# One token tile's query product ahead of the first scores, three tiles' in one row behind them

## The chip, the core and the metric

The kernel runs on one core of one Trainium2 chip. The metric is the device time of one execution in microseconds; the lower the better. Before the change it was 635.88 us, the median of three runs (635.7 to 636.29).

A core has a matrix engine (PE in the profile, with its weight loads shown apart as PEld), a vector engine (DVE), a scalar engine (ACT), a general engine (POOL) and an engine that only issues transfers (SP). Each takes its own instructions in the order in which the program gives them and waits on semaphores for the others.

## What is computed

Eight sequences of 64 tokens, 512 wide, go through three residual blocks: a cross attention against eight contexts of 1601 rows, a linear-attention block with its MLP, and a mixture of eight experts. The change lies in the first block:

```
p       = layernorm(x)                      # 8*64 tokens x 512
trans_q = ctx @ W.T + b                     # never formed: folded into the query
scores  = p @ trans_q.T                     # = (p @ W) @ ctx.T + p @ b
att     = softmax(scores) @ ctx
x       = x + relu(att @ W.T + b)
...                                         # linear attention, MLP, experts
```

The kernel forms `p @ W` once (the query product, `pw_t`) and multiplies it with the context's rows; `p @ b` is one number for each token (`pb`) and comes in as the bias of the copy that takes the scores out of the accumulator banks. All of it is float32.

## The kernel before

**Tiles.** The 512 tokens are four tiles of 128 (two sequences each), numbered t = 0 to 3. The inner dimension 512 is four pieces of 128. The contexts' rows are taken as scores in four groups g of 401 or 398 keys, and as values in three groups of 512 rows and a tail.

**Order.** The order on PE, DVE, ACT, POOL and SP is the order of the program text: it is scheduled by hand, nothing is reordered. Dependences are kept by regions of a tile: a reader of token tile 0 of a buffer does not wait for a later write of tile 1.

**Loads.** x comes in two halves of two tiles, on SP's and on ACT's queue (`xs`, line 101). Then SP loads W (`w_sb`, line 113) and after it everything else in one list (`stream`, `issue_to`): the keys of tile 0, group by group (`ctxT`, two loads of 0.8 MB each, one for each sequence), the bias b after the first group, then keys and rows (`ctx`, two loads of 1 MB) in the order of their use. Context loads go into a ring of 12 buffers (`RING`), and SP issues one when the buffer's former content has been used. Loads also share eight completion semaphores in turn, so that each waits for the landing of the one eight places ahead.

**Start of the work.** Twelve idle matmuls on `ident` (line 224) come first on PE. For each pair of tiles, `statistics` (DVE, then a square root on ACT) and `normalize` (DVE) write `pn`, which is the buffer `xin`; `turn_p` transposes a tile on PE and ACT copies it to `p_t`, which is the buffer `h_t`. W is transposed into four banks (line 405), copied by DVE to `w_t` (line 411); `w_t` is first used at line 547. `pw_half` makes the query product of two tiles for one piece `hc`, 256 columns a matmul, copied by ACT. The first half of the query product lies ahead of the first scores, the second half among the four score groups of tile 0:

```python
    for g in range(4):
        key_group(0, g)
        pw_half(1, g)
```

`key_group(t, g)` (line 441) is the scores of one tile against one group, with ACT's copy under the bias `pb[:, t]`; after g = 3, `softmax` follows. `pb` is computed on DVE after the W copies (line 421). From there `turn_scores` (line 474), `weigh` (line 502, scores times rows), `attended` (line 544) and the later tiles' `key_group`s alternate on PE, with the next block's `values` (line 575) among them.

PSUM is held as two sets of four banks, `mm_bank` and `acc_bank`, given out in turn.

Of the kernel before, what the change touches and what calls it, by code (L numbers as in the profile page):

```python
# [20 lines left out]
P = 128  # L21
B, S, D = 8, 64, 512
LK = 1601
NT = B * S // P
KC = D // P
# [23 lines left out]
def perceiver_kernel(  # L49
# [22 lines left out]
    nc = tc.nc  # L72
# [11 lines left out]
    def mm_bank(name):  # L84
        return ps.tile([P, 512], F32, tag="mm", name=name)

    def acc_bank(name):
        return ps.tile([P, 512], F32, tag="acc", name=name)
# [8 lines left out]


    xs = resid.tile([P, NT, D], F32, name="xs")
    for t, queue in ((0, nc.sync), (2, nc.scalar)):  # L100
        queue.dma_start(xs[:, t : t + 2, :], x[:, t : t + 2, :])
    moe = ctx.enter_context(tc.tile_pool(name="moe", bufs=1))
    mid = ctx.enter_context(ExitStack())
    xinp = mid.enter_context(tc.tile_pool(name="xinp", bufs=1))
# [6 lines left out]
    xa2 = xas.enter_context(tc.tile_pool(name="xa2", bufs=2))  # L111
    w_sb = xa.tile([P, KC, D], F32, tag="w", name="w_sb")
    nc.sync.dma_start(w_sb, xw)
    w_t = xa.tile([P, KC, D], F32, name="w_t")
    xb_bc = const.tile([P, D], F32, name="xb_bc")


    half = H * DH // 2
# [99 lines left out]

    ident = const.tile([P, P], F32, name="ident")
# [133 lines left out]
    def statistics(src, name):  # L353
        st = small.tile([P, 6], F32, tag="st", name=f"st_{name}")
        nc.vector.bn_stats(st, src)
        mv = small.tile([P, 2], F32, tag="mv1", name=f"mv_{name}")
        nc.vector.bn_aggr(mv, st)
        std = small.tile([P, 1], F32, tag="std1", name=f"std_{name}")
        nc.scalar.activation(std, mv[:, 1:2], AF.Sqrt, bias=eps)
        return mv, std  # L360

    def normalize(dst, src, mv, std, name):

        rstd = small.tile([P, 1], F32, tag="rstd1", name=f"rstd_{name}")
        nc.vector.reciprocal(rstd, std)
        nc.vector.tensor_scalar(dst, src, mv[:, 0:1], rstd, ALU.subtract, ALU.mult)


    pn, p_t = xin, h_t
    def turn_p(t):  # L370
        bank = mm_bank(f"tr_p_{t}")
        for c in range(KC):
            nc.tensor.transpose(bank[:, c * P : (c + 1) * P], pn[:, t, c * P : (c + 1) * P], ident)
        nc.scalar.copy(p_t[:, :, t * P : (t + 1) * P], bank.rearrange("p (c q) -> p c q", c=KC))


    pw_t = xa.tile([P, KC, B * S], F32, name="pw_t")

    def pw_half(half, hc):
        cols = slice(half * 2 * P, (half + 1) * 2 * P)  # L380
        bank = mm_bank(f"pw_{half}_{hc}")
        for oc in range(KC):
            nc.tensor.matmul(
                bank[:, : 2 * P],
                w_sb[:, oc, hc * P : (hc + 1) * P],
                p_t[:, oc, cols],
                start=(oc == 0),
                stop=(oc == KC - 1),
            )
        nc.scalar.copy(pw_t[:, hc, cols], bank[:, : 2 * P])  # L390

    issue_to(len(order))

    for t in range(0, NT, 2):
        of = [statistics(xs[:, t + h, :], f"p_{t + h}") for h in range(2)]
        for h in range(2):
            normalize(pn[:, t + h, :], xs[:, t + h, :], *of[h], f"p_{t + h}")
        if t == 0:
            turn_p(0)
            turn_p(1)  # L400

            w_banks = [acc_bank(f"w_t_{hc}") for hc in range(KC)]
            for hc in range(KC):
                for oc in range(KC):
                    nc.tensor.transpose(
                        w_banks[hc][:, oc * P : (oc + 1) * P], w_sb[:, oc, hc * P : (hc + 1) * P], ident
                    )
    pw_half(0, 0)
    pw_half(0, 1)
    for hc in range(KC):  # L410
        nc.vector.tensor_copy(w_t[:, hc, :], w_banks[hc])
    turn_p(2)
    turn_p(3)
    pw_half(0, 2)
    pw_half(0, 3)

    nc.vector.stream_shuffle(xb_bc, xb_in, [0] * 32)
    pb = xa.tile([P, NT], F32, name="pb")
# [22 lines left out]
    def key_group(t, g):  # L441

        if t >= NT:
            return
        if g == 0:
            all_scores[t] = xa2.tile([P, LK], F32, tag="scores", name=f"scores_{t}")
        width = WIDTHS[g]
        sc = acc_bank(f"sc_{t}_{g}")
        keys = [need("ctxT", t, g, h) for h in range(2)]
        for c in range(KC):  # L450
            for h in range(2):
                nc.tensor.matmul(  # L452
                    sc[h * S : (h + 1) * S, :width],
                    pw_t[:, c, (2 * t + h) * S : (2 * t + h + 1) * S],
                    keys[h][:, c, :],
                    start=(c == 0),
                    stop=(c == KC - 1),
                )
        done(*[("ctxT", t, g, h) for h in range(2)])
        nc.scalar.activation(  # L460
            all_scores[t][:, g * SW : g * SW + width], sc[:, :width], AF.Identity, bias=pb[:, t : t + 1]
        )
        if g == 3:
            softmax(t)

    def softmax(t):
        scores = all_scores[t]
        negmax = small.tile([P, 1], F32, tag="negmax", name=f"negmax_{t}")
        nc.vector.tensor_reduce(negmax, scores, AX.X, ALU.max, negate=True)
        rowsum = small.tile([P, 1], F32, tag="rowsum", name=f"rowsum_{t}")  # L470
        nc.scalar.activation(scores, scores, AF.Exp, bias=negmax, accum_out=rowsum)
        all_rinv[t] = rowsum
# [129 lines left out]
            ALU.add,  # L602
        )

    for g in range(4):
        key_group(0, g)
        pw_half(1, g)
    for g in range(2):
        key_group(1, g)
    for t in range(NT):  # L610
# [43 lines left out]
    if True:  # L654
# [178 lines left out]
        of = join(0), join(1)  # L833
# [3 lines left out]
        of = join(2)  # L837
# [7 lines left out]
        of = join(3)  # L845
# [228 lines left out]
    t = NT - 1  # L1074
# [51 lines left out]
    bank = acc_bank("counts")  # L1126
# [632 lines left out]
```

## Time and profile before

| what | value |
|---|---|
| median of three runs | 635.88 us |
| the profiled execution | 636.05 us |
| its span, first to last instruction | 634.3 us |
| PE busy | 617.5 us, 97% |
| DVE, ACT, POOL busy | 29%, 19%, 10% |
| first instruction of real work on PE (`turn_p(0)`) | 8.42 us |
| first scores on PE | 20.66 us |
| start of `turn_scores(0)` on PE | 45.29 us |
| bytes moved | 131.74 MB, mean 208 GB/s over the span |

The profile gives times from the span's start. A float32 matmul shows as two records, a transpose as one. The profile models the end of a matmul, so the pace is read from start to start. PEclk is the clock that the matrix engine was granted, as a share of full speed.

### The profile page before, as it was taken

The page shows a single profiled execution, that of the slowest core. Times are in us where ns is not written, and L with a number is a line of the kernel's source. Part 1 is how long each engine was busy: PE and PEld are TensorE (multiplying, and loading weights), DVE is VectorE, ACT ScalarE, POOL GpSimd, SP SyncE. Part 2 cuts the span into 40 slices and gives each one's busy share as a digit, 9 for nine tenths or more (in the row PEclk, how much of TensorE's full clock was granted, in tenths as well). Part 3 has the DMA queues.
Part 4 walks back from the last instruction along what each step waited for, and adds up shares of the span by engine and source line. Part 5 has one row for each costly group of instructions (what it writes and reads, how often), then busy time and mean ns, then how long its engine had stood idle before and what let it go on. Part 6 is the DMA issues. An engine that isn't in the chain of part 4 may idle for free. (4 is left out here: it accounts for less than half of the span.)

```text
span 634.3 us, 8728 instructions
## 1 busy us (share of the span) xinstructions
PE 617.5 (97%) x3572; PEld 352.2 (56%) x3572; DVE 182.8 (29%) x433; ACT 120.0 (19%) x225; POOL 64.1 (10%) x87
## 2 busy tenths in 40 slices
PE   7999999999999999999999999999999999999994
PEld 7653434343444444455444447966783667775793
DVE  5111322333326888670000026501311101011100
ACT  2241332320132122031111111301101101111110
POOL 4000000000000000050000002241210121301100
PEclk8999999999999999999999999999999999999998
DMA  8999999999421203030312121426890477784711
GB/s 352 409 422 425 423 422 423 425 428 421 199 67 57 77 2 134 0 132 1 122 35 109 67 100 67 168 79 240 300 367 3 165 295 272 298 327 143 296 19 17
DMA packets 23617, 131.74 MB, mean 208 GB/s; under 512 B 4068, under 2 KB 4068, under 8 KB 12168
## 3 DMA queue, kind: packets, MB, share of 16 engines
q1 hardware_dynamic: 19064, 121.80, 48.5%
q0 software_dynamic: 3248, 7.58, 4.8%
q10 hardware_dynamic: 1248, 1.59, 0.8%
q8 instruction: 38, 0.62, 0.4%
q14 instruction: 19, 0.16, 0.1%
HBM read 126.05 MB, written 4.91 MB: 206 GB/s over the span
## 5 line engine op out<-in xcount | busy, mean ns | idle before, releaser
L1261 PEld LDWEIGHTS up<-xgT,e_up 128*128 128x128 f32 x896 | 100.7, 192 | 4.5 <-ACT y_sb L1239 2.5
L1261 PE MATMUL up<-xgT,e_up 128*128 128x128 f32 x896 | 101.6, 275 | 1.0 <-PEq L1589 0.6
L1227 DVE TENSOR_TENSOR mid<-up,act 128x256 f32<-128x256 f32 x38 | 16.1, 425 | 149.2 <-ACT act L1225 149.2
L1275 PE MATMUL y<-e_wo,mid 128*128 128x512 f32 (+1 forms) x144 | 58.8, 547 | 0.0
L858 PE MATMUL hid<-v_sb,w 128*128 128x512 f32 (+2 forms) x144 | 56.6, 545 | 0.0
L879 PE MATMUL mlp<-w,hid_sb 128*128 128x512 f32 x112 | 51.0, 597 | 0.0
L452 PE MATMUL sc<-ctxT,pw_t 128*64 128x401 f32 (+1 forms) x256 | 46.1, 503 | 0.0
L513 PE MATMUL av<-ctx,eT 128*64 128x512 f32 x192 | 43.5, 597 | 0.0
L858 PEld LDWEIGHTS hid<-v_sb,w 128*128 128x128 f32 x144 | 26.2, 190 | 29.1 <-issue 27.3
L1225 ACT ACTIVATE act<-up 128x256 f32<-128x256 f32 x38 | 14.6, 384 | 120.5 <-PE up L1261 96.7
L1275 PEld LDWEIGHTS y<-e_wo,mid 128*128 128x128 f32 x144 | 25.7, 190 | 20.5 <-issue 17.8
L1240 POOL DMA_INDIRECT out_dram<-y_sb,dst_late x12 | 18.3, 1528 | 166.8 <-ACT y_sb L1239 96.8
L879 PEld LDWEIGHTS mlp<-w,hid_sb 128*128 128x128 f32 x112 | 20.7, 190 | 23.5 <-issue 23.4
L873 POOL TENSOR_TENSOR xin<-xin,b_bc 128x512 f32<-128x512 f32 x4 | 5.1, 1268 | 268.4 <-DVE rstd_h L815 265.0
L452 PEld LDWEIGHTS sc<-ctxT,pw_t 128*64 128x64 f32 x256 | 17.5, 136 | 26.0 <-issue 25.8
L666 PE MATMUL wk<-h_t,wk 128*128 128x512 f32 x64 | 29.5, 604 | 0.0
L666 PE MATMUL wq<-h_t,wq 128*128 128x512 f32 x64 | 29.4, 602 | 0.0
L583 PE MATMUL v<-wv,h_t 128*128 128x512 f32 x64 | 29.2, 599 | 0.0
L777 PE MATMUL wo<-wo,a_t 128*128 128x512 f32 x64 | 28.9, 599 | 0.0
L927 DVE TENSOR_TENSOR xs<-mlp,xs 128x512 f32<-128x512 f32 x3 | 2.1, 691 | 86.5 <-PE mlp L879 86.5
L751 DVE RECIPROCAL rden<-rden 128x512 f32<-128x512 f32 x8 | 26.8, 3353 | 0.3
L513 PEld LDWEIGHTS av<-ctx,eT 128*64 128x64 f32 x192 | 13.0, 136 | 24.2 <-issue 23.9
(263 smaller groups left out, 627.8 us busy)
## 6 DMA issues: line engine op xcount, KB each, us to landing
e_up<-in_L_ffn_up_dram SPq DMA_DIRECT2D x32, 1024.0 KB, 5.3
ctx<-in_ctx_dram SPq DMA_DIRECT2D x24, 1024.0 KB, 17.3
ctxT<-in_ctx_T_dram SPq DMA_DIRECT2D x24, 802.0 KB, 13.3
e_wo<-in_L_ffn_wo_dram SPq DMA_DIRECT2D x16, 1024.0 KB, 10.3
w<-in_L_attn_w_dram SPq DMA_DIRECT2D x8, 1024.0 KB, 6.9
ctxT<-in_ctx_T_dram SPq DMA_DIRECT2D x8, 796.0 KB, 16.2
wv<-in_L_attn_wv_dram SPq DMA_DIRECT2D x2, 1024.0 KB
wq<-in_L_attn_wq_dram SPq DMA_DIRECT2D x2, 1024.0 KB, 17.8
```

The costliest lines, as they stand in the source:

```text
L452: nc.tensor.matmul(sc[h * S : (h + 1) * S, :width], pw_t[:, c, (2 * t + h) * S : (2 * t + h + 1) * S], keys[h][:, c, :], start=(c == 0), s ...
L513: nc.tensor.matmul(av[h * S : (h + 1) * S, :], e_t[:, 4 * g + j, h * S : (h + 1) * S], rows[h][:, j, :], start=(g == 0 and j == 0), stop=F ...
L583: nc.tensor.matmul(bank, h_t[:, c, t * P : (t + 1) * P], wv_n[:, c, :], start=(c == 0), stop=(c == KC - 1))
L666: nc.tensor.matmul(bank, w[:, c, (j % 4) * P : (j % 4 + 1) * P], h_t[:, c, :], start=(c == 0), stop=(c == KC - 1),)
L751: nc.vector.reciprocal(rden, rden)
L777: nc.tensor.matmul(wo_banks[t], a_t[:, j, t * P : (t + 1) * P], wo_r[j // 4][:, j % 4, :], start=(j == 0), stop=(j == nj - 1),)
L858: nc.tensor.matmul(hid_banks[f][:, tokens], w[:, c, (f % 4) * P : (f % 4 + 1) * P], h2_t[:, c, tokens], start=(c == 0), stop=(c == KC - 1),)
L879: nc.tensor.matmul(acc[t], hid[:, t * P : (t + 1) * P], need("w2", f // 4)[:, f % 4, :], start=(f == 0), stop=(f == FF // P - 1),)
L1227: nc.vector.tensor_tensor(hid, bank[:, FQ:], act, ALU.mult)
L1240: nc.gpsimd.indirect_dma_start(out=out, out_offset=bass.IndirectOffsetOnAxis(ap=dst[:n, :], axis=0), in_=y_sb[:n, :], in_offset=None, boun ...
L1261: nc.tensor.matmul(bank[:, m * P : (m + 1) * P], up_of[q][:, c, m * P : (m + 1) * P], xg_t[c], start=(c == 0), stop=(c == KC - 1),)
L1275: nc.tensor.matmul(bank[:, :width], h_t[:, j * P : (j + 1) * P], w[:, 2 * (q % 2) + j, n * width : (n + 1) * width], start=(q + j == 0), s ...
```

## The change

- x is loaded in two other parts: token tile 0 alone, ahead of W, and tiles 1 to 3 in one load behind W. Both are on SP's queue; ACT issues none.
- Statistics and normalisation go tile by tile, each with its own trip to ACT, in place of two tiles side by side.
- After tile 0 is normalised, only `turn_p(0)`, the query product of tile 0 (`query(hc, 0, 1)`, 128 columns a matmul) and half of W's transposes (`turn_w(0)`, `turn_w(1)`, copied by ACT) lie ahead of the first scores.
- `key_group(0, 0)` comes next, then `turn_p` of tiles 1 to 3, then `key_group(0, 1)`, then the query product of tiles 1 to 3 in one row (`query(hc, 1, 3)`, 384 columns a matmul), then the other half of W's transposes (copied by DVE), then groups 2 and 3 of tile 0.

```diff
-    for t, queue in ((0, nc.sync), (2, nc.scalar)):
-        queue.dma_start(xs[:, t : t + 2, :], x[:, t : t + 2, :])
+    nc.sync.dma_start(xs[:, :1, :], x[:, :1, :])
...
     nc.sync.dma_start(w_sb, xw)
+    nc.sync.dma_start(xs[:, 1:, :], x[:, 1:, :])
...
-    def pw_half(half, hc):
...
+    def query(hc, first, n):
+        cols = slice(first * P, (first + n) * P)
+        bank = mm_bank(f"pw_{first}_{hc}")
         for oc in range(KC):
             nc.tensor.matmul(
-                bank[:, : 2 * P],
+                bank[:, : n * P],
                 w_sb[:, oc, hc * P : (hc + 1) * P],
                 p_t[:, oc, cols],
...
+        nc.scalar.copy(pw_t[:, hc, cols], bank[:, : n * P])
+
+    def turn_w(hc, copy):
+        bank = acc_bank(f"w_t_{hc}")
+        for oc in range(KC):
+            nc.tensor.transpose(bank[:, oc * P : (oc + 1) * P], w_sb[:, oc, hc * P : (hc + 1) * P], ident)
+        copy(w_t[:, hc, :], bank)
...
-    for t in range(0, NT, 2):
-        of = [statistics(xs[:, t + h, :], f"p_{t + h}") for h in range(2)]
-        for h in range(2):
-            normalize(pn[:, t + h, :], xs[:, t + h, :], *of[h], f"p_{t + h}")
+    for t in range(NT):
+        normalize(pn[:, t, :], xs[:, t, :], *statistics(xs[:, t, :], f"p_{t}"), f"p_{t}")
         if t == 0:
             turn_p(0)
-            turn_p(1)
-
-            w_banks = [acc_bank(f"w_t_{hc}") for hc in range(KC)]
             for hc in range(KC):
-                for oc in range(KC):
-                    nc.tensor.transpose(
-                        w_banks[hc][:, oc * P : (oc + 1) * P], w_sb[:, oc, hc * P : (hc + 1) * P], ident
-                    )
-    pw_half(0, 0)
-    pw_half(0, 1)
-    for hc in range(KC):
-        nc.vector.tensor_copy(w_t[:, hc, :], w_banks[hc])
-    turn_p(2)
-    turn_p(3)
-    pw_half(0, 2)
-    pw_half(0, 3)
+                query(hc, 0, 1)
+            for hc in range(2):
+                turn_w(hc, nc.scalar.copy)
...
-    for g in range(4):
+    key_group(0, 0)
+    for t in range(1, NT):
+        turn_p(t)
+    key_group(0, 1)
+    for hc in range(KC):
+        query(hc, 1, NT - 1)
+    for hc in range(2, KC):
+        turn_w(hc, nc.vector.tensor_copy)
+    for g in range(2, 4):
         key_group(0, g)
-        pw_half(1, g)
```

More of the change, by code (lines that the diff above doesn't have):

```diff
@@ L377, in perceiver_kernel @@
     pw_t = xa.tile([P, KC, B * S], F32, name="pw_t")
-    def pw_half(half, hc):
-        cols = slice(half * 2 * P, (half + 1) * 2 * P)
-        bank = mm_bank(f"pw_{half}_{hc}")
+    def query(hc, first, n):
+        cols = slice(first * P, (first + n) * P)
+        bank = mm_bank(f"pw_{first}_{hc}")
         for oc in range(KC):
             nc.tensor.matmul(
-                bank[:, : 2 * P],
+                bank[:, : n * P],
                 w_sb[:, oc, hc * P : (hc + 1) * P],
@@ L389, in pw_half @@
             )
-        nc.scalar.copy(pw_t[:, hc, cols], bank[:, : 2 * P])
+        nc.scalar.copy(pw_t[:, hc, cols], bank[:, : n * P])
[4 more added lines that the diff above has]
+        copy(w_t[:, hc, :], bank)
     issue_to(len(order))
-    for t in range(0, NT, 2):
-        of = [statistics(xs[:, t + h, :], f"p_{t + h}") for h in range(2)]
-        for h in range(2):
-            normalize(pn[:, t + h, :], xs[:, t + h, :], *of[h], f"p_{t + h}")
+    for t in range(NT):
+        normalize(pn[:, t, :], xs[:, t, :], *statistics(xs[:, t, :], f"p_{t}"), f"p_{t}")
         if t == 0:
             turn_p(0)
-            turn_p(1)
-            w_banks = [acc_bank(f"w_t_{hc}") for hc in range(KC)]
             for hc in range(KC):
-                for oc in range(KC):
-                    nc.tensor.transpose(
-                        w_banks[hc][:, oc * P : (oc + 1) * P], w_sb[:, oc, hc * P : (hc + 1) * P], ident
-                    )
-    pw_half(0, 0)
-    pw_half(0, 1)
-    for hc in range(KC):
-        nc.vector.tensor_copy(w_t[:, hc, :], w_banks[hc])
-    turn_p(2)
-    turn_p(3)
-    pw_half(0, 2)
-    pw_half(0, 3)
+                query(hc, 0, 1)
+            for hc in range(2):
+                turn_w(hc, nc.scalar.copy)
     nc.vector.stream_shuffle(xb_bc, xb_in, [0] * 32)
```

## The prediction, made before the changed kernel ran

> **What bounds the kernel now.** I read the page first, then PE's timeline up to the first softmax, the early stretches in windows, and last the transfers of the scores' stage.
>
> ```profile
> span 634.3 us, 8728 instructions
> PE 617.5 (97%) x3572; PEld 352.2 (56%) x3572; DVE 182.8 (29%) x433; ACT 120.0 (19%) x225; POOL 64.1 (10%) x87
> ...
> DMA  8999999999421203030312121426890477784711
> ```
>
> PE is the bound nearly everywhere, so what PE saves early arrives at the end, unless something else ends last in between. The DMA row names the candidate: the transfers are full for ten slices, to about 165 us. PE's timeline:
>
> ```profile
> 1.45 4.78 PE L224 MATMUL idle<-ident 128*128 128x128 f32 x24 [1.45 <-POOL ident masks.py:199]
> 8.42 1.77 PE L373 MATMUL tr_p<-ident,xin 128*128 128x128 f32 x8 [2.20 <-DVE xin L366]
> 9.98 2.97 PE L405 MATMUL w_t<-ident,w_sb 128*128 128x128 f32 x16
> 12.78 3.62 PE L383 MATMUL pw<-h_t,w_sb 128*128 128x256 f32 x16
> 16.24 1.04 PE L373 MATMUL tr_p<-ident,xin 128*128 128x128 f32 x8
> 17.11 3.62 PE L383 MATMUL pw<-h_t,w_sb 128*128 128x256 f32 x16
> 20.66 2.92 PE L452 MATMUL sc<-ctxT,pw_t 128*64 128x401 f32 x16
> 23.51 1.99 PE L383 MATMUL pw<-h_t,w_sb 128*128 128x256 f32 x8
> ...
> 39.74 5.62 PE L452 MATMUL sc<-ctxT,pw_t 128*64 128x401 f32 x32
> 45.29 1.53 PE L485 MATMUL et<-ident,scores 128*128 128x128 f32 x12
> ...
> 85.69 2.85 PE L452 MATMUL sc<-ctxT,pw_t 128*64 128x398 f32 x16
> ```
>
> PE waits once, 2.2 us for tile 0's normalised rows, and is dense from 8.42 us. Columns of the windows: busy us and records of PE, PEld, DVE, ACT, POOL, then granted clock, DMA share, GB/s.
>
> ```profile
> 5.31:8.72 3.41, 1.21 (x11) 1.02 (x11) 2.55 (x8) 0.59 (x2) 2.41 (x13) 1.00 1.02 427
> 8.72:12.13 3.41, 3.41 (x19) 3.23 (x18) 2.86 (x9) 1.55 (x4) 0.00 (x0) 0.50 1.02 424
> 623.12:626.53 3.41, 2.36 (x11) 1.73 (x10) 0.48 (x1) 0.47 (x1) 0.00 (x0) 1.00 0.00 0
> 626.53:629.94 3.41, 0.00 (x0) 0.00 (x0) 0.00 (x0) 0.00 (x0) 1.55 (x1) 1.00 0.34 27
> ```
>
> The stretch behind the wait runs at half clock: 3.41 us that do 1.7 us of work. The last two rows are the counterexample: a stretch with 2.36 us busy did not lower the next.
>
> The transfers, in SP's timeline and in its waits from 82 to 85 us:
>
> ```profile
> 64.32 2.81 SPq L201 DMA_DIRECT2D ctxT<-in_ctx_T_dram  x2
> ...
> 84.34 0.33 SPq L201 DMA_DIRECT2D ctx<-in_ctx_dram  x1
> ```
>
> ```profile
> SPq L201 <- DMA ctxT<-in_ctx_T_dram: 3.0, 2, 1.5
> ```
>
> The keys of group (2, 3) are the two issues from 64.32 us. SP's issue at 84.34 waited for the landing of the second, so that came at 84.3. PE uses it at 85.69. Followed over every key and row load up to 165 us in this way, this is the least slack: 1.4 us.
>
> **The change, step by step.** All durations are of this execution; I follow it to the start of `turn_scores(0)`, 45.29 before.
>
> *Tile 0's load.* A lone 1 MB load on an idle SP queue (`e_up`, issued at 241.7) lands after 4.8 us. Tile 0 has 0.79 MB less, 1.85 us at 424 GB/s: 2.95 us, so about 3.8. [...] The upper bound is the old landing, 6.0. I take 3.8, the nearest row. DVE and ACT then need, by the first tile's rows without the second tile between, 0.73 (statistics), 0.21, 0.32 (root on ACT), 0.17, 0.61 (normalise, handoff): 2.04, so 5.9. The idle matmuls end at 6.1, so PE starts there in both cases: 2.3 us earlier than 8.42.
>
> *The first row.* Four transposes at 0.11 (eight took 16.24 to 17.11), ACT's copy 0.59 and the handoffs: `query` starts at 7.5, PE idle 0.9. W lands before that: it landed at 8.5 and has 0.79 MB less ahead, 6.6. 32 records of 128 columns at 0.11 (the 128 records of L1261 from 604.04 take 14.53): 3.6, to 11.1. Eight transposes of W, 0.9: 12.0. The first keys have the same bytes ahead as before and land at 12.4 (SP's issue at 12.46 waited for them): scores from 12.45, 2.85 a group (20.66 to 23.51), to 15.3. PE idle 0.4.
>
> *Tiles 1 to 3.* On ACT the root of tile 1 now lies behind the four query copies and two W copies: it starts at 12.7. Tile 1 is normalised at 13.8, and each next tile takes a whole trip, 0.69 + 0.22 + 0.33 + 0.66 = 1.9: 15.7 and 17.6. On PE, `turn_p(3)` waits for that, 1.4 us idle. Group (0, 1) follows, 18.15 to 21.0. DVE's shuffle (0.76) and first bias column (0.70) end at 19.1; ACT's first score copy waits for it, and behind it in ACT's order stand the three `p_t` copies (0.48 apart): 21.2. So the row starts at 21.3, 0.3 idle.
>
> *The row and the rest.* 32 records of 384 columns: the pace is 0.216 at 256 columns and 0.429 at 512, so 0.322, 10.3 us, to 31.6. W's other transposes 0.9, then four groups as before (two took 39.74 to 45.29 with the switch, two more 5.4): `turn_scores(0)` at 43.5. **Gain on PE: 1.8 us.** As an account: start 2.3, half clock gone 1.7, fewer switches between 64 and 128 columns 0.7 (0.34 a pair, from the 4.78 us period less 2.70 and 1.73), query product 13.9 against 13.8, new idle time 3.0: 1.6, which agrees to 0.2.
>
> *Costed at nothing.* SP's extra x issue (0.44) moves the key issues, covered by a queue in which the first key load waits 8.6 us; uncovered it costs 0.44. ACT's x issue goes, in its idle start. W's late halves are first used at 70 us. `softmax(0)` has lost the query product behind group (0, 3): its exponential ends at 42.4, 1.1 us ahead of need, and beyond that it costs one for one.
>
> *A rule against the row.* "TensorE: Matmul & The Clock Gate" (HAM oscillation) warns of idle gaps over about 3.4 us. By that neither the old gap of 2.2 us nor the new one of 1.4 lowers the clock, the half-clock stretch has another cause and may stay: the gain would be 0.1. In the row a gap of 2.2 is followed by 0.50. I go by the row: it goes with the gap.
>
> *What is late next.* PE would reach group (2, 3) at 83.9, but its keys land at 84.3 whatever PE does: the stream before it has the same bytes and starts as early. With a handoff of 0.06 and a first record 0.06 longer PE keeps 1.3 us, 1.4 if SP's first packet is slightly ahead of ACT's old one. I take 1.4. The later slacks (2.1 us and more) then hold, and PE carries it to the end.
>
> The profiled execution was 636.05 us, its span 634.3 and 1.75 around it, 0.17 above the median: 634.65 against it, **634.5 against the median**.
>
> **Rivals.**
>
> 1. *The stream does not bind.* The new start lets it run 0.4 us ahead. Then the whole 1.8 us stays: 634.1. Against it: DMA share 1.01 to 1.03 from 5 us on leaves nothing to catch up.
> 2. *The clock falls in the new wait.* The 1.4 us for tile 3 in one stretch leave about 2.1 us busy, between 1.21 (fell) and 2.36 (did not). It costs 1.7 us: 635.8, no change.
> 3. *Slower: the normalisation chain starves PE.* Tiles 1 to 3 make three trips DVE, ACT, DVE one after the other, behind ACT's copies. The price is the lateness of tile 3 one for one, and from about 0.7 us of it the stretch falls under 1.5 us busy and half clock adds 1.7. It decides at 1.4 us, 0.47 a trip: 1.8 - 1.4 - 1.7 = -1.3, so 637.2, and at 2.4 us 638.2. For it: handoffs are priced at 0.03 to 0.05 us each, with no room. Against it: DVE and ACT have nothing else to do there.
>
> **How the numbers follow.** The likeliest case (0.60) is a gain of 0.9 to 2.0 us, 633.9 to 635.0. What a measurement tells from no change is 0.2%, 1.27 us, and the forecast lies just beyond it: of the 0.60 I give 0.47 to faster, 0.13 to the same. Rival 1 has 0.07 (faster), rival 2 0.10 (same), rival 3 0.23 (slower). Faster 0.54, same 0.23, slower 0.23. The range runs from 633.7, rival 1 with 0.4 us more, to 637.2, where rival 3 decides; beyond lie some 0.18.
>
> **What would show it.** Right: `turn_p(0)` near 6.1 us, no half-clock stretch before 20 us, a wait of `turn_p(3)` near 17.6, `turn_scores(0)` near 43.5, and a wait of PE for the keys of group (2, 3) near 84.3. Wrong: tile 0 landing after 5 us, PE's first wait on DVE over 2 us behind group (0, 0), a clock of 0.50 there, or group (2, 3) starting with its keys long landed.

## The result, and the profile after

| | before | after |
|---|---|---|
| median, 22 runs each in turn | 635.97 us | 636.83 us |
| ratio, 95% interval | | 1.0015 (1.0008 to 1.0021) |
| profiled execution | 636.05 us | 637.04 us |
| its span | 634.3 us | 635.3 us |
| `turn_scores(0)` on PE | 45.29 us | 44.22 us |
| second key load of group (2, 3) landed | 84.3 us | 86.0 us |
| start of the next block's `wq` product on PE | 173.28 us | 173.65 us |

The change costs 0.9 us. That is inside what the prediction counts as no change, but the interval lies wholly on the slower side: there is no gain of 1.4 us. The page of the changed kernel:

```profile
span 635.3 us, 8725 instructions
...
PE 617.7 (97%) x3572; PEld 350.2 (55%) x3572; DVE 182.0 (29%) x431; ACT 121.0 (19%) x227; POOL 64.4 (10%) x87
...
PEclk9999999999999999999999999999999999999998
DMA  8999999999521204030312121427890477884711
GB/s 336 379 425 424 422 424 423 425 428 420 238 67 55 79 2 134 0 133 1 127 31 107 67 100 67 167 78 239 302 367 3 164 296 273 295 326 142 298 19 17
```

PE's busy time is what it was (617.5). The change stands in the last row: the first two slices moved 336 and 379 GB/s, and the eleventh, where the score stage's stream runs out, 238. The same row before:

```profile
GB/s 352 409 422 425 423 422 423 425 428 421 199 67 57 77 2 134 0 132 1 122 35 109 67 100 67 168 79 240 300 367 3 165 295 272 298 327 143 296 19 17
```

Bytes have moved from the start of the stream to its end. PE's timeline, to be laid beside the prediction's:

```profile
1.44 4.98 PE L224 MATMUL idle<-ident 128*128 128x128 f32 x24 [1.44 <-POOL ident masks.py:199]
6.66 0.66 PE L373 MATMUL tr_p<-ident,xin 128*128 128x128 f32 x4 [0.23 <-DVE xin L366]
7.99 3.84 PE L383 MATMUL pw<-h_t,w_sb 128*128 128x128 f32 x32 [0.68 <-ACT h_t L374]
...
12.63 3.44 PE L444 MATMUL sc<-ctxT,pw_t 128*64 128x401 f32 x16
...
18.38 0.66 PE L373 MATMUL tr_p<-ident,xin 128*128 128x128 f32 x4 [1.28 <-DVE xin L366]
...
21.90 10.59 PE L383 MATMUL pw<-h_t,w_sb 128*128 128x384 f32 x32
...
44.22 1.53 PE L477 MATMUL et<-ident,scores 128*128 128x128 f32 x12
...
84.85 0.83 PE L444 MATMUL sc<-ctxT,pw_t 128*64 128x398 f32 x2
85.27 0.59 PE L505 MATMUL av<-ctx,eT 128*64 128x512 f32 x1
86.01 2.89 PE L444 MATMUL sc<-ctxT,pw_t 128*64 128x398 f32 x14
```

PE works faster up to 44.22, a lead of 1.07 us. At group (2, 3), where before ran without a break from 85.69, it now stops after two records and goes on at 86.01. (The record of L505 between them is of the product that stands ahead of the group in the program.) SP's timeline and its waits at that place (85.5 to 86.5 us):

```profile
66.08 2.80 SPq L201 DMA_DIRECT2D ctxT<-in_ctx_T_dram  x2
...
86.03 2.76 SPq L201 DMA_DIRECT2D ctx<-in_ctx_dram  x2
```

```profile
SPq L201 <- DMA ctxT<-in_ctx_T_dram: 1.5, 1, 1.5
```

These are the two rows that the prediction showed at 64.32 and 84.34. SP's issue at 86.03 waited for the landing of the second key load: it came at about 86.0, not at 84.3. The lead of 1.07 turned into a loss of 0.37 by the start of `wq`. The rest of the profile's difference, 0.6 us of span, lies in the experts (a wait for gathered rows at 424 us, a branch at 571), and these waits differ by as much between executions of one kernel: two more profiles of the kernel before, +0.03 and -0.26 at `wq` against the first, stood at +0.44 and -0.78 behind them. They are not put down to the change.

Where the stream loses its bytes is seen in windows (columns as in the prediction's; the last two are DMA share and GB/s). Before:

```profile
2.00:3.00 1.00, 1.00 (x7) 1.00 (x6) 0.00 (x0) 0.53 (x1) 1.00 (x3) 1.00 0.55 115
3.00:4.00 1.00, 1.00 (x7) 1.00 (x7) 0.00 (x0) 0.20 (x1) 0.93 (x5) 1.00 0.96 397
...
25.00:31.00 6.00, 6.00 (x33) 3.00 (x33) 0.00 (x0) 1.34 (x3) 0.00 (x0) 1.00 1.03 419
```

After:

```profile
2.00:3.00 1.00, 1.00 (x7) 1.00 (x6) 0.00 (x0) 0.10 (x1) 1.00 (x3) 1.00 1.01 221
3.00:4.00 1.00, 1.00 (x7) 1.00 (x7) 0.00 (x0) 0.20 (x1) 0.93 (x5) 1.00 0.56 137
...
25.00:31.00 6.00, 6.00 (x20) 3.52 (x19) 0.00 (x0) 1.23 (x3) 0.00 (x0) 1.00 0.94 333
```

There are two losses. At 3 to 4 us the transfers are half idle (137 against 397 GB/s): tile 0's short load is all but done, and of the 16 packets with which W starts ten come only from 3.7 us on. At 25 to 31 us the rate is 333 against 419. Summed over the packets from the span's start, the stream is behind before by 0.26 MB at 6 us, 0.25 at 25 and 0.73 at 31, and then stays there (0.72 at 80 us). 0.72 MB at 424 GB/s is 1.7 us, which is the lateness of the keys: 86.0 less 84.3.

### The profile page after: what moved, and what is told of

Read it like the earlier page. It is cut to its first block, busy times and chain, and to the rows that moved or that the text cites. A ratio compares the mean times of both kernels' runs of the same rounds, so it can differ in the third digit from the quotient of the medians.

```text
span 635.3 us, 8725 instructions
## 1 busy us (share of the span) xinstructions
PE 617.7 (97%) x3572; PEld 350.2 (55%) x3572; DVE 182.0 (29%) x431; ACT 121.0 (19%) x227; POOL 64.4 (10%) x87
## 3 DMA queue, kind: packets, MB, share of 16 engines
q10 hardware_dynamic: 1104, 1.07, 0.5%
## 5 line engine op out<-in xcount | busy, mean ns | idle before, releaser
L505 PE MATMUL av<-ctx,eT 128*64 128x512 f32 x192 | 44.6, 597 | 0.0
L505 PEld LDWEIGHTS av<-ctx,eT 128*64 128x64 f32 x192 | 13.2, 136 | 25.1 <-issue 23.9
## 6 DMA issues: line engine op xcount, KB each, us to landing
ctxT<-in_ctx_T_dram SPq DMA_DIRECT2D x24, 802.0 KB, 15.1
e_wo<-in_L_ffn_wo_dram SPq DMA_DIRECT2D x16, 1024.0 KB, 10.2
```

The lines of the kernel that those rows point to most:

```text
L505: nc.tensor.matmul(av[h * S : (h + 1) * S, :], e_t[:, 4 * g + j, h * S : (h + 1) * S], rows[h][:, j, :], start=(g == 0 and j == 0), stop=F ...
```

## The experiments

My theory after reading this: the load stream, late by two separate losses, takes PE's gain, and each loss is worth its own time. Rivals: the losses are chance; the row of 384 columns or the new order disturbs the stream; the gain is lost behind the first block; or the gain on PE was never worth its time. In what follows "lag" is the bytes by which SP's and ACT's queues stand behind the first profile of before (in the six runs with the small loads on POOL's queue, 0.07 MB of it are those loads, moved elsewhere), and "lead" is PE's against that profile, at `turn_scores(0)` (45.29) and at `wq` (173.28).

| run | loss to 6 us, MB | lag at 31 us, MB | lead at `turn_scores(0)`, us | lead at `wq`, us | median, us | ratio to before (95%) |
|---|---|---|---|---|---|---|
| after_again | 0.26 | 0.53 | 1.08 | -1.09 | 636.93 | 1.0014 (1.0007 to 1.0021) |
| order_alone | none | none | -2.18 | -2.18 | 638.07 | 1.0029 (1.0019 to 1.0038) |
| rest_on_act | none | none | -2.18 | -2.18 | 637.26 | 1.0013 (1.0006 to 1.0020) |
| one_queue | 0.18 | 0.57 | 1.62 | -1.14 | 636.21 | 1.0003 (0.9995 to 1.0011) |
| tile0_on_act | 0.23 | 0.27 | -3.91 | -3.91 | 640.53 | 1.0068 (1.0055 to 1.0082) |
| tile0_act_wv | 0.21 | 0.27 | -4.27 | -4.27 | 640.62 | 1.0071 (1.0057 to 1.0085) |
| smalls_on_pool | 0.17 | 0.18 | 1.17 | 0.67 | 636.18 | 0.9998 (0.9990 to 1.0007) |
| wv_later | 0.20 | 0.52 | 1.19 | 0.62 | 635.59 | 0.9994 (0.9986 to 1.0002) |
| wv_smalls | 0.26 | 0.30 | 0.88 | 0.87 | 635.38 | 0.9992 (0.9983 to 1.0000) |
| before_wv_smalls | none | 0.01 | 1.40 | 1.39 | 635.28 | 0.9990 (0.9982 to 0.9999) |
| one_queue_wv_smalls | 0.18 | 0.20 | 1.99 | 1.65 | 634.56 | 0.9981 (0.9971 to 0.9992) |
| early_roots | 0.23 | 0.26 | 2.67 | 1.58 | 634.57 | 0.9979 (0.9970 to 0.9987) |
| before_warm | none | 0.15 | 1.61 | 0.88 | 639.93 | 1.0065 (1.0051 to 1.0079) |
| before_warm_edits | none | 0.02 | 1.40 | 1.39 | 637.45 | 1.0022 (1.0013 to 1.0031) |
| before_wide | none | 0.20 | 1.32 | 0.50 | 635.80 | 0.9999 (0.9990 to 1.0008) |
| before_pad | none | 0.02 | -0.95 | -0.96 | 639.43 | 1.0052 (1.0038 to 1.0066) |

The leads and lags are of one profiled execution each, the medians of several.

### after_again: chance or not

The changed kernel once more, with no edit.

> The changed kernel once more, for a second profile of it. In the first, PE reached turn_scores(0) 1.1 us earlier than before (44.2 against 45.3), but the keys of group (2, 3) landed at 86.0 against 84.3. The stream had fallen behind by 0.27 MB at 3 to 5 us (0.64 us) and by another 0.46 MB at 25 to 31 us (1.1 us). Theory 'start': the first loss belongs to the load order and is here again, keys of (2, 3) at 84.9 or later. Theory 'row': the second loss belongs to the 384-column row, which runs from 22 to 32 us, and is here again, keys at 86.0. Theory 'chance': the second loss is one of this execution alone and is absent, keys at 84.9. The time, about 636.8, tells nothing between them.

Both losses come again, the first of the same size (0.26 MB), the second smaller (0.30 MB from 25 to 31 us, against 0.48). Group (2, 3) goes on at 86.74, and PE stands 1.09 us behind before at `wq`. So neither is chance, though the second varies in size.

### order_alone and rest_on_act: the order or the loads

order_alone is the changed order with the old loads of x:

```diff
-    nc.sync.dma_start(xs[:, :1, :], x[:, :1, :])
+    for t, queue in ((0, nc.sync), (2, nc.scalar)):
+        queue.dma_start(xs[:, t : t + 2, :], x[:, t : t + 2, :])
...
-    nc.sync.dma_start(xs[:, 1:, :], x[:, 1:, :])
```

> The order of the changed kernel with the loads of before (halves of x on SP and ACT). Theory 'start': no loss at 3 to 5 us. Theory 'row': the second loss of about 0.46 MB at 25 to 31 us is here, since the row is. 'Chance': it is not. PE starts near 8.1 and the stretch behind its wait falls to half clock as in before: turn_scores(0) near 46 to 47, so the time is about 636.7 to 637.7 by PE alone, whatever the stream does.

rest_on_act keeps tile 0 alone on SP's queue and loads tiles 1 to 3 at the same time on ACT's:

```diff
+    nc.scalar.dma_start(xs[:, 1:, :], x[:, 1:, :])
...
-    nc.sync.dma_start(xs[:, 1:, :], x[:, 1:, :])
```

> Tiles 1 to 3 of x go on ACT's queue at the start, beside tile 0 on SP's; the rest as changed. Theory 'start' (one queue starts the stream 0.64 us late): the stream is as early as before at 6 us, tile 0 lands near 5.0, W near 8.4, turn_scores(0) starts near 44.8. Keys of (2, 3) at 84.3 without a second loss: gain 0.5 us on before, 635.5. With theory 'row' added (1.1 us lost at 25 to 31 us): keys at 85.4, gain 0.3 us, 635.7. Rival 'size' (the 256 KB load with its 2 KB packets, not the one queue, starts the stream late): the 0.27 MB are missing again at 5 us.

In both the stream loses nothing up to 31 us, with the 384-column row in place: the row does not disturb the stream. But in both tile 0 is late (`turn_p(0)` at 8.28), and the clock falls to half for 3.4 us behind it (from 9.6 and 10.2 us), so that PE is 2.2 us late at `turn_scores(0)` in both profiles (not in all of their executions, as `before_again` below shows). The new order without an early tile 0 is worth less than nothing; and whatever shares the transfers with tile 0 at the start takes its time.

### one_queue: the loads without the new order

The order before, x's tiles 0 and 1 ahead of W and tiles 2 and 3 behind it, all on SP's queue:

```diff
-    for t, queue in ((0, nc.sync), (2, nc.scalar)):
-        queue.dma_start(xs[:, t : t + 2, :], x[:, t : t + 2, :])
+    nc.sync.dma_start(xs[:, :2, :], x[:, :2, :])
...
     nc.sync.dma_start(w_sb, xw)
+    nc.sync.dma_start(xs[:, 2:, :], x[:, 2:, :])
```

> The order of before, with x's halves both on SP: tiles 0 and 1, W, tiles 2 and 3. Theory 'start' as one queue: the stream lacks about 0.27 MB at 5 us and keys of (2, 3) land at 84.9; PE starts earlier (tiles 0 and 1 near 5.2, turn_p(0) near 7.5) but can keep no more than 0.7 us of it at group (2, 3): 635.3 to 635.9. Rival 'size': 4 KB packets start the stream as before, keys at 84.3, gain up to 1.3 us, 634.7. Theory 'row': no loss at 25 to 31 us, since there is no row.

Both losses are there without the new order and without the 256 KB load (0.18 MB, then 0.39 more between 25 and 31 us). There is no half-clock stretch, and PE leads by 1.62 us at `turn_scores(0)`, more than in the changed kernel; it loses all of it and 1.1 us more waiting for keys and rows. So neither loss needs this change's order on PE. The first goes with the way x is loaded. For the second this run does not part the loads from an early PE, which it has too; `smalls_on_pool` and `before_wide` below do.

### tile0_on_act and tile0_act_wv: the first loss

The changed kernel with tile 0's load on ACT's queue, so that W is at the head of SP's; the second one with `wv_later`'s edit too (below).

```diff
-    nc.sync.dma_start(xs[:, :1, :], x[:, :1, :])
+    nc.scalar.dma_start(xs[:, :1, :], x[:, :1, :])
```

> The changed kernel with tile 0's load on ACT's queue; W, the other tiles and all else on SP's. So far: kernels with all of x on SP's queue start the stream 0.18 to 0.26 MB late, those with two queues do not; the loss at 25 to 31 us goes with the first (changed kernel and one_queue), not with the 384-column row (order_alone and rest_on_act have the row and no loss). Theory 'start': with two queues both losses go, tile 0 lands near 4.6, turn_scores(0) near 44.2, keys of (2, 3) at 84.3 and PE keeps about 1.1 to 1.3 us: 634.8. Rival 'size' (the 256 KB load with 2 KB packets itself starts the stream late): the lag at 6 us is again 0.2 MB or more, keys at 85 to 86, 636 to 637.

> Both: tile 0's load on ACT's queue and wv[0] behind the keys of (2, 3). Theories 'start' and 'stream binds' together: no wait of PE on the stream, PE keeps what it has at turn_scores(0), 1.1 to 1.3 us: 634.7 to 634.9. If only one holds, as in the run of that one.

A miss: the stream lags by 0.2 to 0.3 MB all the same, and tile 0 lands at 7.19 us in place of 4.56, because its packets of 2 KB run among W's packets of 8 KB: the last of them ends at 6.31 us, in the changed kernel at 4.22. PE's timeline shows the price:

```profile
9.29 1.12 PE L373 MATMUL tr_p<-ident,xin 128*128 128x128 f32 x4 [3.28 <-DVE xin L366]
```

PE waits 3.28 us, two stretches at half clock follow (8.3 to 15.1 us), and the time is 4.4 us above before; with PE that late, the edit of the load list does nothing. Two queues at the start are thus not what avoids the first loss. What holds most of W's first packets back to 3.7 to 4.2 us in the changed kernel was not found; every arrangement tried either had the gap, or had other bytes in flight beside tile 0 and tile 0 late.

### smalls_on_pool: the second loss

The changed kernel with five small loads (the columns of biases, `col`, and the contexts' last rows, four loads into `v_sb`) issued by POOL in place of SP:

```diff
-                nc.sync.dma_start(t_, src)
+                (nc.gpsimd if (key == "col" or key[0] == "last") else nc.sync).dma_start(t_, src)
```

> The changed kernel with the five small loads (four of context_last, one of columns) on POOL's queue, which have semaphores of their own; in SP's list they hold five of the eight semaphores that SP's loads take in turn, from 13 to 25 us. Theory 'semaphores': SP's issues of group (1, 0) no longer wait for one late engine at 22.3 us, the second loss (0.3 to 0.46 MB at 25 to 31 us) goes, the first stays: keys of (2, 3) at 84.9, gain on before 0.7 us, 635.3. Rival: the second loss has to do with the start alone, and is here again: keys at 85.5 to 86, 636.3 to 636.9.

The second loss is gone: the lag is 0.17 MB at 6 us and 0.18 at 31. The window of smalls_on_pool:

```profile
25.00:31.00 6.00, 6.00 (x20) 3.49 (x19) 0.00 (x0) 1.12 (x3) 0.00 (x0) 1.00 1.01 416
```

SP's timeline shows how. Before:

```profile
20.30 5.92 SPq L201 DMA_DIRECT2D ctxT<-in_ctx_T_dram  x4
```

In the changed kernel:

```profile
13.19 4.43 SPq L194 DMA_DIRECT2D v_sb<-in_ctx_last_dram  x4
19.06 0.33 SPq L194 DMA_DIRECT2D col<-in_columns_dram  x1
22.27 4.83 SPq L201 DMA_DIRECT2D ctxT<-in_ctx_T_dram  x4
27.19 1.18 SPq L201 DMA_DIRECT2D ctx<-in_ctx_dram  x2
28.47 1.35 SPq L201 DMA_DIRECT2D ctxT<-in_ctx_T_dram  x2
```

In smalls_on_pool:

```profile
12.94 4.76 SPq L201 DMA_DIRECT2D ctxT<-in_ctx_T_dram  x4
20.34 2.29 SPq L201 DMA_DIRECT2D ctx<-in_ctx_dram  x2
24.20 2.25 SPq L201 DMA_DIRECT2D ctxT<-in_ctx_T_dram  x2
```

The small loads take five of the eight completion semaphores in turn, and SP waits for a landing ahead of each. In the changed kernel the keys of group (1, 0) could only be issued from 22.27 us, because one of the 16 engines landed its part of an earlier load 1.2 us behind the other 15; the queue then has too little in it and runs at 333 GB/s. With the five loads elsewhere SP issues the same keys from 12.94 us and never falls behind. That the small loads make the second loss possible is shown. PE still loses 0.5 us in group (2, 3) (3.34 us for 2.85), and of its lead of 1.17 us it keeps 0.67 at `wq`. The time did not follow as far as that: 0.9998.

What makes the one engine late is a fetch of instructions: a packet of 16 KB that holds it for 1.1 us. It is in every trace, and its time parts the 14 traces in which SP issues the small loads:

| | second loss (6) | none (8) |
|---|---|---|
| runs | after, after_again, one_queue, wv_later, before_warm, before_wide | before (3), order_alone, rest_on_act, tile0_on_act, tile0_act_wv, before_pad |
| fetch starts, us | 17.3 to 19.3 | 19.7 to 23.2 |
| last of 16 parts of the key load lands behind the rest by, us | 0.8 to 1.2 | under 0.2 |
| keys of (1, 0) issued, us | 21.3 to 22.3 | 20.2 to 21.2 |
| lead at `turn_scores(0)`, us | 1.07 to 1.62 | -4.27 to 0.26 |

So the second loss goes with an early PE and not with the loads of x: an early PE comes with an early fetch, and the early fetch delays the landing for which SP's issue waits. That PE's pace draws the fetch forward fits all 14 traces, but is inferred: the profile does not say whose instructions are fetched.

### wv_later: take bytes out from ahead of the keys

The changed kernel with the first value weight (1 MB) moved behind the keys of (2, 3) in the load list:

```diff
+        if t == 1:
+            stream(("wv", 0), wv[0])
...
-        if t == 0:
-            stream(("wv", 0), wv[0])
```

> The changed kernel with the 1 MB load of wv[0], first used at 88 us, put behind the keys of (2, 3) in SP's list; everything else as changed. Theory 'stream binds': the keys of (2, 3) land 2.5 us earlier, 83.5, PE does not wait for them and passes there 1.1 us ahead of before (84.6); the next least slack, the keys of (3, 1), leaves it 0.4 to 1.1 us: 634.9 to 635.6. Rival 'PE pays elsewhere': the wait at (2, 3) goes, and the time stays at 636.8.

The losses stay (lag 0.52 MB at 31 us), the keys of (2, 3) come in time (the group starts at 84.50 and runs without a break), and PE's lead, 1.19 us there, is still 1.06 at the second group of tile 3, where the next keys are late by 0.44. The time falls by 1.2 us against the changed kernel, in the ratio to before from 1.0014 to 0.9994.

### wv_smalls, before_wv_smalls, one_queue_wv_smalls: both edits

> The changed kernel with both edits of the load list: the first value weight moved behind the keys of group (2, 3), and the small loads (bias rows, last context rows) on POOL's queue. If both losses of the load stream are what cancels PE's gain, PE keeps its lead of 1.05 us at turn_scores(0) through the score groups of tiles 2 and 3 (group (2, 3) at 84.5 without a wait, group (3, 1) at about 98.5) up to the stage of the values, and the time is 634.9. If only one of the two edits can act (the loss behind it is the same microsecond), it stays at 635.6. If the gain is lost elsewhere, behind 170 us, it stays at 636.

> The kernel before with the same two edits of the load list. In the kernel before PE waited for none of these loads (least slack 1.4 us), so by the theory that the edits only repair what the changed kernel is late in, nothing moves: 636.0, ratio 0.999 to 1.001. If the two edits are worth something by themselves (fewer issues in front of the transfers of the later stages), it is faster by the same 0.5 to 1 us as the changed kernel was, 635.2.

> The order before, with tiles 0 and 1 of x ahead of W and tiles 2 and 3 behind it, all on SP's queue, and the two edits of the load list. With the loads alone PE was at turn_scores(0) at 43.67, a lead of 1.6 us over the kernel before, and lost it waiting for the keys of group (2, 3). If the stream alone took it, the lead now stays: group (2, 3) at about 84.1, time 634.4 to 634.8, ahead of the changed kernel with the same edits. If the stream binds next at (3, 1), it keeps about 0.6: 635.5.

wv_smalls keeps all of its lead to `wq` (0.88, then 0.87); the time is 635.38, 1.5 us better than the changed kernel, and 0.5 short of what I expected. Up to `wq`, the stream is thus what took PE's lead.

before_wv_smalls was to stay at 636.0, and came to 635.28: a miss. Its profile holds the reason for a part: there is no half-clock stretch in it, and PE leads by 1.4 us and keeps it. By the mark of the mean clock (`before_again` below) 4 of its 12 runs had no such stretch, median 634.88 us, and 8 had one, 635.50. The 35 runs of before beside them give 635.89 (14) and 635.81 (21). So an early PE seems to pay with the edits, by 0.6 us, and not without them; behind a stretch the edits themselves are worth some 0.3. The run also limits what wv_smalls shows: with the same edits in both, the changed kernel (635.38) is not faster than the kernel before (635.28). The edits restore the lead on PE; that the change would then be worth its lead in time is not shown.

one_queue_wv_smalls did what was expected: lead 1.99, 1.65 of it left at `wq`, 634.56. The old order on PE with x in two parts on one queue is as good as anything found here.

### early_roots: the wait for tile 3

wv_smalls with the roots of tiles 1 to 3 placed on ACT between the query copies and the W copies:

```diff
+    tokens(0)
+    turn_p(0)
+    query(0, 0, 1)
+    tokens(1)
+    for hc in range(1, KC):
+        query(hc, 0, 1)
+    tokens(2)
+    turn_w(0, nc.scalar.copy)
+    tokens(3)
+    turn_w(1, nc.scalar.copy)
```

(`tokens(t)` is statistics and normalisation of one tile.)

> The changed kernel with the two edits of the load list, and the roots of tiles 1 to 3 placed on ACT between the query copies and the W copies rather than behind them all. If the queue in front of the roots is what makes turn_p(3) wait (1.28 us) and the row start late, the wait falls under 0.3 us and turn_scores(0) starts at about 42.8, a lead of 2.4; with a stream that follows, the time is 633.6. If the stream binds at (2, 3) or (3, 1) again, the lead at the start of the values is at most about 1.2 and the time about 635. If three trips DVE, ACT, DVE set the wait, not the queue, turn_p(3) still waits over 0.8 us.

```profile
15.87 1.53 PE L373 MATMUL tr_p<-ident,xin 128*128 128x128 f32 x12
17.33 3.05 PE L449 MATMUL sc<-ctxT,pw_t 128*64 128x401 f32 x16
20.30 10.59 PE L383 MATMUL pw<-h_t,w_sb 128*128 128x384 f32 x32
...
42.62 1.53 PE L482 MATMUL et<-ident,scores 128*128 128x128 f32 x12
...
83.58 2.85 PE L449 MATMUL sc<-ctxT,pw_t 128*64 128x398 f32 x16
...
98.05 3.41 PE L449 MATMUL sc<-ctxT,pw_t 128*64 128x401 f32 x16
```

The twelve transposes run in one piece: the wait of 1.28 us for tile 3 and the gap ahead of the row are gone, so it was the queue on ACT that made them, and not the three trips. The lead is 2.67 us at `turn_scores(0)`, of which 1.58 is left at `wq`: 0.56 goes by (2, 3), and the group at 98.05 takes 3.41 us rather than 2.92, held by its keys. The stream is the bound again, and 634.57 is no better than one_queue_wv_smalls, whose lead at `turn_scores(0)` was 0.7 us less. Both beat the kernel before (by 1.3 us) and the changed one (by 2.3).

### before_warm, before_wide, before_pad: what the half-clock stretch was worth

The largest term of the forecast gain, next to the earlier start, was the 1.7 us of half clock. To take it away in the old order, PE is kept busy longer at the start. before_warm does it by more idle matmuls, before_warm_edits the same on before_wv_smalls:

```diff
-NIDLE = 12
+NIDLE = 18
```

> The kernel before with 18 idle matmuls at the start in place of 12, so that PE is busy up to about 7.5 us, its wait for tile 0 falls to 0.5 to 1 us and no half-clock stretch follows. turn_scores(0) should start near 43.6 (45.29 less 1.7). By the forecast's cap (keys of group (2, 3) at 84.3) 1.35 us of that arrive: 634.6. If the stream of the kernel before is late as soon as PE is early, or something further on takes it, nothing arrives: 635.9.

> The same with the first value weight later in the load list and the small loads on POOL's queue. PE's 1.7 us should stay through (2, 3) and (3, 1): 634.2. If only part of the runs of the kernel before have the half-clock stretch, the difference to before_wv_smalls (635.28) is about half of 1.7 us, 634.5; if all have it, 633.6.

The stretch is gone and `turn_scores(0)` starts 1.61 us earlier, but both are slower than without the edit, by 3.9 and 2.2 us. PE stands still in the experts, twice in the middle of a run of matmuls, with nothing released. So two kernels separate the two things that the edit does. before_pad adds the six instructions with no more columns in all:

```diff
-NIDLE = 12
+NIDLE = 18
...
-        nc.tensor.matmul(idle_bank[:, :P], ident, ident, start=True, stop=True)
+        nc.tensor.matmul(idle_bank[:, :85], ident, ident[:, :85], start=True, stop=True)
```

> The kernel before with 18 idle matmuls of 85 columns in place of 12 of 128: six more instructions, the same idle work, the half-clock stretch stays. If the added instructions cause the two stalls in the experts, they appear near 425 and 550 us, 1.1 to 1.9 us each, and the time is 638.5 to 640. If the stalls came with the earlier arrival of PE, they are absent, and the time is 636.0.

PE's waits of before_pad behind 175 us (us in total, times, longest), and its timeline there:

```profile
PE up L1313 <- issue: 2.1, 1, 2.1
PE y L1275 <- issue: 1.4, 1, 1.4
```

```profile
425.49 1.92 PE L1313 MATMUL up<-e_up,xgT 128*32 128x512 f32 x16 [0.57 <-ACT xgT L1219]
429.55 2.79 PE L1313 MATMUL up<-e_up,xgT 128*32 128x512 f32 x12 [2.13 <-issue]
```

Both stalls are there, at the same matmuls as in before_warm, with PE late rather than early. So they belong to the six instructions, not to the time at which PE arrives. No profile without the six instructions shows either. From `wq` to the end of the stalls PE loses 2.7 us in before_warm, 2.9 in before_warm_edits and 4.7 in before_pad against the kernel before; the medians rise by 3.9, 2.2 and 3.4, so the stalls are not of one size in all executions. (before_pad's narrow matmuls also brought the clock up only at 13.1 us, which makes PE 0.95 us late at the start.) They are probably waits for instructions: in the three traces each of the six stalls begins within 0.7 us of the end of a 16 KB fetch of instructions. But other fetches pass without a stall, and no view names the wait.

before_wide has the longer idle work with as many instructions on PE:

```diff
+    nc.vector.memset(w_t[:, 0, :192], 0.0)
...
-        nc.tensor.matmul(idle_bank[:, :P], ident, ident, start=True, stop=True)
+        nc.tensor.matmul(idle_bank[:, :192], ident, w_t[:, 0, :192], start=True, stop=True)
```

> The kernel before with its 12 idle matmuls 192 columns wide in place of 128 (on a cleared piece of w_t): the same number of instructions on PE, idle work up to about 7.5 us, no half-clock stretch. turn_scores(0) at about 43.7. If six added instructions caused the two stalls in the experts, they are gone here. If the stretch is worth its time in the old order, less what the load stream takes (a lead of 0.9 us was left at the start of the values in before_warm), the time is 635.1; if the stream or something further on takes it all, 636.0.

```profile
1.45 6.44 PE L225 MATMUL idle<-w_t,ident 128*128 128x192 f32 x24 [1.45 <-POOL ident masks.py:199]
8.57 1.32 PE L374 MATMUL tr_p<-ident,xin 128*128 128x128 f32 x8 [0.69 <-DVE xin L367]
...
43.97 1.53 PE L486 MATMUL et<-ident,scores 128*128 128x128 f32 x12
...
84.38 0.50 PE L453 MATMUL sc<-ctxT,pw_t 128*64 128x398 f32 x1
84.39 0.59 PE L514 MATMUL av<-ctx,eT 128*64 128x512 f32 x1
84.71 3.31 PE L453 MATMUL sc<-ctxT,pw_t 128*64 128x398 f32 x15
```

The eight transposes take 1.32 us rather than 1.77: full clock. PE leads by 1.32 us at `turn_scores(0)`, the group (2, 3) is cut up by waits, the stream lags by 0.20 MB at 31 us, and 0.50 us is left at `wq`. The median is that of before (0.9999, 0.9990 to 1.0008). Here nothing of the change is in place. The old kernel's load stream is late when PE is early, here and in before_warm (the fetch of instructions starts at 19.26 and 17.33 us, in the first profile of before at 21.22), and a lead of 1.3 us is worth nothing that was measured; the 0.5 us left at `wq` would be inside the interval.

### before_again and before_again2

> The kernel before once more, for its profile. If the half-clock stretch is in each execution, PEclk is 0.50 in a stretch of 3.41 us behind the wait again and turn_scores(0) starts at 45.3. If it depends on where the clock's stretches fall, a profile whose first full-clock stretch begins later than about 6.3 us has none, starts turn_scores(0) at 43.6 and then waits for keys at (2, 3).

> A second profile of the kernel before, for the same question: PEclk 0.50 for 3.41 us and turn_scores(0) at 45.3 with the first full-clock stretch beginning before about 6.3 us, neither of them with it beginning later.

Both have the half-clock stretch (from 9.0 and 8.1 us, 3.4 us long), and `turn_scores(0)` at 45.33 and 45.03; the first full-clock stretch began at 5.5 and 4.7 us. Neither began late enough to try the second half of the expectation. Two other kernels with the old order did: in before_wv_smalls and one_queue the first full-clock stretch began at 6.9 and 6.6 us, and behind idle gaps of 1.13 and 1.43 us no half clock followed.

What the stretch is worth can be read from the mean clock of each run. In the 20 profiles it is 0.990 to 0.994 where there is a half-clock stretch besides the one at the end of every span (8), and 0.995 to 0.997 where there is none (12). Runs parted by this mark:

| kernel | runs at 0.995 or more: median, us | runs under 0.995: median, us |
|---|---|---|
| before, all runs beside the experiments | 67: 636.04 | 84: 635.99 |
| order_alone | 4: 636.63 | 10: 638.37 |
| rest_on_act | 10: 636.25 | 12: 637.58 |

By this the kernel before runs without the stretch in nearly half of its executions, and they are no faster; where PE is late, the stretch costs 1.3 to 1.7 us. The mark is a mean, and not a view of each run.

## Why the prediction was wrong

**Right.** The bound after the change was named (the keys of group (2, 3)), and so was the place. PE's steps came as forecast, in order: first row to 11.66 (11.1), scores at 12.63 (12.45), the wait of `turn_p(3)` 1.28 us at 18.38 (1.4 near 17.6), the row from 21.90 (21.3) at 10.4 us (10.3), no stretch at half clock. The half clock went with the gap, here and in before_wide. The gap's length is not the measure, though. The rule of the Trainium skill's "TensorE: Matmul & The Clock Gate" (HAM oscillation) warns of idle gaps over about 3.4 us; here half clock followed gaps of 2.20 us and, in rest_on_act, 1.35, while none followed 1.43 us in one_queue. The busy time of the first full-clock stretch parts all 20 profiles: behind 0.74 to 1.47 us of 3.41 the clock fell (7), behind 1.85 or more it did not (13).

**Wrong in size.** Tile 0 landed at 4.56 us, not 3.8. The nearest row, a lone load on an idle queue less its bytes at full rate, was too good by 0.75 us. DVE and ACT took 2.1 us from there, as priced, and `turn_p(0)` started at 6.66, not at 6.1. Only 0.23 us of this was the wait for tile 0: the idle matmuls themselves ended at 6.42 (in after_again at 6.84, with no wait left). ACT's copies handed the lateness on to the roots (tile 1's at 13.26, not 12.7) and so to tile 3, and with some 0.15 us more in the row the gain on PE was 1.07 us, not 1.8.

**Overvalued.** The 1.7 us of half clock, the largest term after the earlier start, were counted from one profile as if each execution of the kernel before had them. By the mean clocks nearly half had not, and were no faster.

**The step that failed** is "its keys land at 84.3 whatever PE does: the stream before it has the same bytes and starts as early". It has the same bytes, and its first packets start earlier, but it does not run full: 0.26 MB are lost at 3 to 4 us and 0.3 to 0.5 MB at 25 to 31. The landing moved to 86.0. "Whatever PE does" is the other half of the error: the second loss goes with an early PE, with the old loads too. I had priced the change of the x loads as an extra issue of 0.44 us under a cover of 8.6 us, and looked at when loads are issued, not at whether the queue has packets to move, nor at what the landings ahead of an issue do to it. "DMA share 1.01 to 1.03 from 5 us on" described the old loads, and did not hold for the new ones. With 1 MB taken from ahead of the keys (wv_later), with the second loss gone (smalls_on_pool), and with both (wv_smalls), PE stands 0.62, 0.67 and 0.87 us ahead at `wq`, not 0.37 behind.

**The rivals.** Rival 1, a stream that does not bind, went the other way: it bound harder. Rivals 2 and 3 did not occur; normalisation starved PE for 1.28 us, within the forecast. The slower end came from a mechanism that I had not among the rivals: a stream made late by the change itself. That 636.83 lies inside the stated range is luck: its upper end was set for rival 3. And before_wide shows that even the gain as forecast would not have arrived whole: in the old order a lead of 1.3 us shrank to 0.5 by `wq`.

**Open.** What delays W's first packets; whose instructions the early fetch brings; and what the change would be worth in time with a stream that is never late.

## What to carry to other kernels

When the compute engine is ahead of a load stream by little, a gain on the engine is worth at most that slack, and the slack itself is to be forecast anew: ask of each window of the stream whether the queue has bytes in flight, what each issue waits for, and what a late landing holds up. A short first load gets its consumer started early and leaves the transfers half idle behind it. Price the edit on the stream (a big load moved behind the keys that bind, small loads taken off the queue's semaphores) along with the edit on the engine: here the edits of the stream alone took 0.6 us off the kernel before, and the edit on the engine alone added 0.9. And count a stretch of low clock as a gain only after asking in how many executions it occurs.

## What the runs showed of the hardware

- Six more matmuls at the start of PE's program cost 2 to 4 us (2.2, 3.4 and 3.9 in three kernels), in stalls of 1.1 to 2.1 us inside two runs of matmuls 420 and 540 us later, each time the same runs. Kernels with a changed number of instructions are not to be compared to the microsecond without looking for such stalls.
- A stall of this kind can be followed by half clock as the wait at the start was. In before_pad, a stretch with 1.31 of 3.40 us busy is followed by one at 0.50:

```profile
426.10:429.50 3.40, 1.31 (x15) 0.15 (x4) 0.00 (x0) 0.00 (x0) 2.01 (x2) 1.00 0.62 197
429.50:432.90 3.40, 3.35 (x16) 0.59 (x16) 0.00 (x0) 0.00 (x0) 0.00 (x0) 0.50 0.20 60
```

- Two loads on two queues ran with their packets mixed: 256 KB in 2 KB packets beside 1 MB in 8 KB packets landed at 7.19 us, alone at the head of one queue at 4.56.
- A fetch of instructions is one packet of 16 KB that takes 1.1 us on one of the 16 transfer engines. A load behind it lands with one part 0.8 to 1.2 us late, and with it what waits for the whole load.
- In all profiles but before_pad's, the clock came up to full at 4.5 to 6.9 us from the span's start, differing from one execution to the next; the end of the twelve idle matmuls moves with it, from 5.9 to 6.9 us.
